# The last sample's store behind the section, and SyncE's closing waits in a section of their own

## The chip, the cores and the metric

The kernel runs on one core of a Trainium2 chip. The core has a matrix engine (TensorE), a vector engine (VectorE), a scalar engine (ScalarE), GpSimd and SyncE, which issues transfers and waits. Each engine runs its own instruction stream; semaphores order them against each other. Transfers between the chip's memory and the core's on-chip memory (SBUF) run on 16 DMA engines. The metric is the time of one execution on the device in microseconds (us); lower is better. The kernel before takes 327.56 us, the median of three runs (327.24 to 327.79).

## What is computed

`x` has 128 samples of 128 channels by 1024 time steps in float32. Each sample names one of eight subjects, and each subject has a 128 x 128 weight matrix. Every sample is multiplied by its subject's matrix, and the product is added to the sample:

```python
def _L0_cond_ref(x, subjects, weights):
    B, C, D, T, N_SUBJECTS = (128, 128, 128, 1024, 8)
    w = weights[subjects]
    out = jnp.einsum('bct,bcd->bdt', x, w)
    return out
x = x + _L0_cond_ref(x, itok_B_0_7, L0_cond_weights)
```

A sample is 512 KB. Some 67 MB are read and 67 MB written, whatever the kernel does.

## The kernel before

The kernel is written in one block, a critical section, in which every semaphore and every wait is set by hand. The layer around it (the tile context) adds what stands before and behind a section: at the end of a section SyncE raises a mark, every other engine drains and raises a count, and SyncE collects these counts; at the end of the program all engines meet twice in a barrier.

Work goes in tiles of four samples (`H * G`, two pairs of two), so there are `NT` = 32 tiles. Twelve tiles (`SLOTS`) can be held in SBUF at once; tile i uses slot i mod 12. A unit of work is one pair, but for the first pair, which is taken sample by sample.

- SyncE issues the loads (`load`, L123), one 512 KB transfer for each sample, in order. From tile 12 on it first waits until the slot's last store has landed (L171).
- GpSimd copies each sample's weight matrix into one of four small buffers (L202); the first copy of a pair also waits for the pair's loads.
- TensorE multiplies (L212): two matmuls of 512 columns for each sample, each recorded as two instructions, a pair into one of two PSUM buffers.
- VectorE adds the product to the sample in place, in SBUF (L223), and raises `s_added`.
- ScalarE waits for `s_added` and issues the stores (`store`, L56 is the line that records each transfer of either kind). Tile 0 is stored in three pieces, every other tile in one transfer of 2 MB when its second pair is done. So tile 31 goes as one transfer of 2 MB, sent when the very last addition is done.

Each slot has two semaphores, `s_pair[k][0]` and `s_pair[k][1]`. Loads and stores raise them by 16 for each transfer; `emptied` and `loaded` work out the values to wait for. A tile's store raises the second one.

At the end of the section SyncE waits until the last twelve tiles' stores have landed (L233). In the profile these waits stand on L233, the closing of the section on L141 (SyncE's branch out of the section, its mark, everybody's drain, SyncE's collection) and the end of the program on L257 (the two barriers and the clearing of the semaphores between them). The order of the instructions on each engine is the order in which they are written here; no scheduler moves anything inside the section.

Of the kernel before, what the change touches and what calls it, by code (L numbers as in the profile page):

```python
# [26 lines left out]
G = 2  # L30
H = 2
# [3 lines left out]
SLOTS = 12  # L35
# [5 lines left out]
DMA = 16  # L41
# [7 lines left out]
def transfer(nc, engine, out, in_):  # L49

    later, nc._always_lower_symbolic_ap = nc._always_lower_symbolic_ap, False
    ins, outs = engine.lower_ap_dma(in_), engine.lower_ap_dma(out)
    nc._always_lower_symbolic_ap = later
    return engine.add_instruction(  # L56
        mybir.InstDMACopy(
            name=nc.get_next_instruction_name(),
            engine=engine.engine,
            ins=ins,  # L60
            outs=outs,
            mode="Copy",
            cce_op=ALU.bypass,
            queue=QUEUES[engine.engine],
        )
    )


@with_exitstack
def kernel(  # L70
    ctx: ExitStack,
    tc: tile.TileContext,
    x: bass.AP,
    subjects: bass.AP,
    weights: bass.AP,
    out: bass.AP,
):
    nc = tc.nc
    B, C, T = x.shape
    S, _, D = weights.shape  # L80
    NT = B // (G * H)

    def sbuf(name, *shape, dtype=F32):
        return ctx.enter_context(nc.sbuf_tensor(name, list(shape), dtype)).ap()

    given, near, wrap, index = (
        sbuf(name, 1, B, dtype=I32) for name in ("given", "near", "wrap", "index")
    )
    w_all = sbuf("w_all", C, S, D)
    ws = [sbuf(f"w{i}", C, 1, D) for i in range(W_SLOTS)]  # L90
    zeros = sbuf("zeros", C, N)
    xs = [sbuf(f"x{i}", C, H * G, T) for i in range(SLOTS)]
    ps = [
        ctx.enter_context(nc.psum_tensor(f"ps{i}", [D, G, T], F32)).ap() for i in range(P_SLOTS)
    ]

    s_given = tc.alloc_semaphore("s_given")
    s_wall = tc.alloc_semaphore("s_wall")
    s_index = tc.alloc_semaphore("s_index")
    s_zeros = tc.alloc_semaphore("s_zeros")  # L100
    s_copied = tc.alloc_semaphore("s_copied")
    s_product = tc.alloc_semaphore("s_product")
    s_added = tc.alloc_semaphore("s_added")

    s_pair = [[tc.alloc_semaphore(f"s_pair{i}_{h}") for h in range(H)] for i in range(SLOTS)]


    s_first = tc.alloc_semaphore("s_first")

    def emptied(i, h):  # L110


        turns = i // SLOTS
        return (DMA * G + (DMA if h == H - 1 else 0)) * turns

    def loaded(i, q):

        if i + q == 0:
            return s_first, DMA
        h = q // G  # L120
        return s_pair[i % SLOTS][h], emptied(i, h) + (DMA if i + h == 0 else DMA * G)

    def load(engine, i, q):  # L123
        k, h = i % SLOTS, q // G
        transfer(
            nc,
            engine,
            xs[k][:, q, :],
            x[i * H * G + q].rearrange("(a r) t -> a (r t)", r=ROWS),
        ).then_inc(s_first if i + q == 0 else s_pair[k][h], DMA)  # L130

    def store(i, q0, q1):
        k, b = i % SLOTS, i * H * G
        transfer(
            nc,
            nc.scalar,
            out[b + q0 : b + q1].rearrange("g d t -> d g t"),
            xs[k][:, q0:q1, :].rearrange("d (o g) t -> d o (g t)", g=min(G, q1 - q0)),
        ).then_inc(s_first if i + q1 == 1 else s_pair[k][(q1 - 1) // G], DMA)

    with tc.tile_critical():  # L141

        nc.scalar.dma_start(given, subjects.rearrange("(o b) -> o b", o=1)).then_inc(s_given, DMA)

        nc.vector.memset(zeros, 0.0).then_inc(s_zeros, 1)  # L145
        nc.tensor.wait_ge(s_zeros, 1)
        for _ in range(IDLE):
            nc.tensor.matmul(  # L148
                ps[P_SLOTS - 1][:, G - 1, :N], zeros[:, :D], zeros, start=True, stop=True
            )  # L150

        nc.vector.wait_ge(s_given, DMA)
        nc.vector.tensor_scalar(near, given, -S, S - 1, ALU.max, ALU.min).then_inc(s_index, 1)  # L155
        nc.vector.wait_ge(s_index, 1)
        nc.vector.tensor_scalar(wrap, near, 0, S, ALU.is_lt, ALU.mult).then_inc(s_index, 1)  # L157
        nc.vector.wait_ge(s_index, 2)
        nc.vector.tensor_tensor(index, near, wrap, ALU.add).then_inc(s_index, 1)  # L159
        nc.gpsimd.wait_ge(s_index, 3)  # L160


        load(nc.sync, 0, 0)
        nc.sync.dma_start(w_all, weights.rearrange("s c d -> c s d")).then_inc(s_wall, DMA)
        for i in range(NT):
            k = i % SLOTS
            if i == SLOTS:
                nc.sync.wait_ge(s_first, 2 * DMA)
                nc.sync.wait_ge(s_pair[0][0], emptied(i, 0))
            if i >= SLOTS:  # L170
                nc.sync.wait_ge(s_pair[k][H - 1], emptied(i, H - 1))  # L171
            for q in range(H * G):
                if i + q:
                    load(nc.sync, i, q)


        units = [(0, g, g + 1) for g in range(G)]
        units += [(j // H, j % H * G, (j % H + 1) * G) for j in range(1, NT * H)]
        for u, (i, q0, q1) in enumerate(units):
            k, j = i % SLOTS, i * H + q0 // G  # L180
            p = ps[j % P_SLOTS]

            ahead = j < P_SLOTS
            if ahead:
                nc.tensor.wait_ge(*loaded(i, q0))
            for q in range(q0, q1):
                b = i * H * G + q
                if b % R == 0:  # L190
                    _, subject = nc.values_load_multi_w_load_instructions(
                        index[0:1, b : b + R],
                        engines=[mybir.EngineType.Pool],
                        min_val=0,
                        max_val=S - 1,
                        skip_runtime_bounds_check_because="the index is clamped on the chip above",
                    )
                if b == 0:
                    nc.gpsimd.wait_ge(s_wall, DMA)
                if not ahead and q == q0:  # L200
                    nc.gpsimd.wait_ge(s_added, u - P_SLOTS + 1)
                copy = nc.gpsimd.tensor_copy(  # L202
                    ws[b % W_SLOTS], w_all[:, bass.ds(subject[b % R], 1), :]
                )
                if not ahead and q == q0:
                    copy.wait_op(*loaded(i, q0), "sem-ge")
            copy.then_inc(s_copied, 1)

            nc.tensor.wait_ge(s_copied, u + 1)
            for q in range(q0, q1):  # L210
                for t in range(0, T, N):
                    mm = nc.tensor.matmul(  # L212
                        p[:, q % G, t : t + N],
                        ws[(i * H * G + q) % W_SLOTS][:, 0, :],
                        xs[k][:, q, t : t + N],
                        start=True,
                        stop=True,
                    )
            mm.then_inc(s_product, 1)

            mine = xs[k][:, q0:q1, :]
            nc.vector.wait_ge(s_product, u + 1)
            nc.vector.tensor_tensor(  # L223
                mine, p[:, q0 % G : q0 % G + q1 - q0, :], mine, ALU.add
            ).then_inc(s_added, 1)

            if i == 0 or q1 == H * G:
                nc.scalar.wait_ge(s_added, u + 1)
                store(i, q0 if i == 0 else 0, q1)


        for i in range(NT - SLOTS, NT):
            nc.sync.wait_ge(s_pair[i % SLOTS][H - 1], emptied(i + SLOTS, H - 1))  # L233


# [25 lines left out]
```

## Time and profile before

| | |
|---|---|
| median of the runs | 327.56 us (327.24 to 327.79, three runs) |
| the profiled execution | 327.34 us |
| its span, first to last instruction | 325.6 us |
| DMA, mean over the span | 134.85 MB, 414 GB/s |
| last load issued by SyncE | 260.8 us after the start |
| last addition on VectorE | 276.1 to 278.4 us |
| last store issued by ScalarE | 295.1 us |
| a 2 MB store, issue to landing | 46.4 us (median) |
| a matmul of 512 columns; an addition of a pair | 605 ns; 2259 ns |

The span is counted from the program's first instruction to its last; what lies around it (1.8 us here) is the same kind of work for every program. A store's time to landing is long because hundreds of transfers' pieces stand in the same queues: it is time in a queue, and not the time that the bytes take. From 278.4 us on no engine computes: what is left of the span is stores that are still queued, and the end of the program.

### The profile page before, as it was taken

The page shows a single profiled execution, that of the slowest core. Times are in us where ns is not written, and L with a number is a line of the kernel's source. Part 1 is how long each engine was busy: PE and PEld are TensorE (multiplying, and loading weights), DVE is VectorE, ACT ScalarE, POOL GpSimd, SP SyncE. Part 2 cuts the span into 40 slices and gives each one's busy share as a digit, 9 for nine tenths or more (in the row PEclk, how much of TensorE's full clock was granted, in tenths as well). Part 3 has the DMA queues.
Part 4 walks back from the last instruction along what each step waited for, and adds up shares of the span by engine and source line. Part 5 has one row for each costly group of instructions (what it writes and reads, how often), then busy time and mean ns, then how long its engine had stood idle before and what let it go on. Part 6 is the DMA issues. An engine that isn't in the chain of part 4 may idle for free.

```text
span 325.6 us, 1600 instructions
## 1 busy us (share of the span) xinstructions
PE 240.8 (74%) x518; PEld 94.5 (29%) x518; DVE 148.0 (45%) x69; POOL 34.3 (11%) x132
## 2 busy tenths in 40 slices
PE   7999988898888887888988888888888858000000
PEld 3444333333333332333333333333333323000000
DVE  1466655555555555454555555555554453200000
POOL 1011111011111111111011111111111010000000
PEclk9999999999999999999999999999999999755555
DMA  6999999999999999999999999999999999999994
GB/s 242 400 435 416 427 416 427 433 426 420 425 430 426 417 428 425 430 419 425 427 424 423 420 434 422 426 427 426 425 422 434 413 428 426 426 428 426 428 425 199
DMA packets 16058, 134.85 MB, mean 414 GB/s; under 512 B 2609, under 2 KB 3634, under 8 KB 3890
## 3 DMA queue, kind: packets, MB, share of 16 engines
q1 hardware_dynamic: 7184, 67.64, 49.7%
q10 hardware_dynamic: 8866, 67.11, 49.1%
q8 instruction: 4, 0.07, 0.1%
q14 instruction: 4, 0.03, 0.0%
HBM read 67.63 MB, written 67.11 MB: 414 GB/s over the span
## 4 chain that ended last, share of the span: by engine, by line
PE 41%; DVE 21%; issue 18%; POOL 5%; POOLq 1%; DVEq 0%; SPq 0%
PE ps L212 40%; DVE x L223 21%; POOL w L202 5%; PE ps L148 2%; POOLq L202 1%; DVE zeros L145 0%; DVEq L257 0%; SPq L141 0%
## 5 line engine op out<-in xcount | busy, mean ns | idle before, releaser
L212 PE MATMUL ps<-x,w 128*128 128x512 f32 x512 | 235.5, 605 | 33.6 <-POOL w L202 33.6
L223 DVE TENSOR_TENSOR x<-ps,x 128x2048 f32<-128x2048 f32 (+1 forms) x65 | 146.8, 2259 | 128.7 <-PE ps L212 128.7
L212 PEld LDWEIGHTS ps<-x,w 128*128 128x128 f32 x512 | 92.7, 190 | 177.0 <-issue 93.6
L202 POOL COPY w<-w_all 128x128 f32 x128 | 34.1, 296 | 237.8 <-DMA x<-in_x_dram 217.1
L148 PE MATMUL ps<-zeros 128*128 128x512 f32 x6 | 5.5, 1088 | 1.7 <-DVE zeros L145 1.7
L148 PEld LDWEIGHTS ps<-zeros 128*128 128x128 f32 x6 | 1.8, 328 | 3.7 <-issue 2.1
L145 DVE MEMSET zeros<- 128x512 f32 x1 | 0.5, 485 | 1.1 <-SPq L141 1.1
L155 DVE TENSOR_SCALAR near<-given 1x128 int32<-1x128 int32 x1 | 0.2, 214 | 0.5 <-DMA given<-in_itok_B_dram 0.5
L159 DVE CUSTOM_DVE_ANT_0 index<-near,wrap 1x256 uint16<-1x256 uint16 x1 | 0.3, 280 | 0.0
L157 DVE TENSOR_SCALAR wrap<-near 1x128 int32<-1x128 int32 x1 | 0.2, 216 | 0.0
L248 POOL MEMSET const-float32-0.0<- 128x1 f32 x1 | 0.1, 99 | 0.2 <-issue 0.2
L248 POOL MEMSET const-bfloat16-1.0<- 128x1 bf16 x1 | 0.1, 102 | 0.0
L248 POOL MEMSET const-uint8-127<- 128x1 uint8 x1 | 0.1, 102 | 0.0
L248 POOL MEMSET const-float32-1.0<- 128x1 f32 x1 | 0.1, 99 | 0.0
## 6 DMA issues: line engine op xcount, KB each, us to landing
x<-in_x_dram SPq DMA_DIRECT2D x128, 512.0 KB, 32.1
out_dram<-x ACTq DMA_DIRECT2D x31, 2048.0 KB, 46.4
out_dram<-x ACTq DMA_DIRECT2D x2, 512.0 KB, 11.8
out_dram<-x ACTq DMA_DIRECT2D x1, 1024.0 KB, 14.9
w_all<-in_L_cond_weights_dram SPq DMA_DIRECT2D x1, 512.0 KB, 4.8
given<-in_itok_B_dram ACTq DMA_DIRECT2D x1, 0.5 KB
```

The costliest lines, as they stand in the source:

```text
L145: nc.vector.memset(zeros, 0.0).then_inc(s_zeros, 1)
L148: nc.tensor.matmul(ps[P_SLOTS - 1][:, G - 1, :N], zeros[:, :D], zeros, start=True, stop=True)
L155: nc.vector.tensor_scalar(near, given, -S, S - 1, ALU.max, ALU.min).then_inc(s_index, 1)
L157: nc.vector.tensor_scalar(wrap, near, 0, S, ALU.is_lt, ALU.mult).then_inc(s_index, 1)
L159: nc.vector.tensor_tensor(index, near, wrap, ALU.add).then_inc(s_index, 1)
L202: copy = nc.gpsimd.tensor_copy(ws[b % W_SLOTS], w_all[:, bass.ds(subject[b % R], 1), :])
L212: mm = nc.tensor.matmul(p[:, q % G, t : t + N], ws[(i * H * G + q) % W_SLOTS][:, 0, :], xs[k][:, q, t : t + N], start=True, stop=True,)
L223: nc.vector.tensor_tensor(mine, p[:, q0 % G : q0 % G + q1 - q0, :], mine, ALU.add).then_inc(s_added, 1)
L248: nc = _bacc.Bacc("TRN2", target_bir_lowering=False, num_devices=1)
```

## The change

There are three edits. The last tile is no longer stored in one transfer: its first pair goes when that pair is done (1 MB), the third sample goes by itself (512 KB), and the fourth sample, sample 127, isn't stored in the section. SyncE's waits for the stores leave the first section and become a second section, `waits`, with one wait more for the last tile's first pair. Sample 127 is stored by a `dma_start` of ScalarE outside both sections, so that its semaphore belongs to the tile context, and the end of the program waits for it. A dependence for the scheduler alone says on which side of `waits` it stands.

```diff
-            if i == 0 or q1 == H * G:
+            if i == 0 or q1 == H * G or i == NT - 1:
                 nc.scalar.wait_ge(s_added, u + 1)
-                store(i, q0 if i == 0 else 0, q1)
-
-
+                store(i, q0 if i in (0, NT - 1) else 0, q1 - (b == B - 1))
+
+
+
+    with tc.tile_critical() as waits:
         for i in range(NT - SLOTS, NT):
             nc.sync.wait_ge(s_pair[i % SLOTS][H - 1], emptied(i + SLOTS, H - 1))
+        nc.sync.wait_ge(s_pair[(NT - 1) % SLOTS][0], emptied(NT - 1 + SLOTS, 0) + DMA)
+    last = nc.scalar.dma_start(out[B - 1], xs[(NT - 1) % SLOTS][:, H * G - 1, :])
+
+    tc.add_manual_dep(
+        last.ins,
+        waits.name,
+        mybir.DependencyInfo(mybir.DependencyClass.NoSync, mybir.DependencyReason.SCHED_ONLY),
+        reason="the end of the program waits for it",
+    )
```

In the built program the instructions stand as follows. SyncE: loads, the closing of the first section, the waits for stores (those of tiles 20 to 30, of the last tile's first pair and of sample 126), the closing of the second section, one drain that waits for sample 127's semaphore, the barriers. ScalarE: its stores, the drain that closes the first section, the store of sample 127 behind a wait for SyncE's count that the first section is closed, the barriers. The other engines pass one more branch.

## The prediction

> **What bounds the kernel now.** I read the page first (span, the row of DMA shares, the queues), then a table of windows over the last 26 us, then SyncE's list of waits, then the instructions of the three lines that end the program.
>
> ```profile
> span 325.6 us, 1600 instructions
> ...
> PE 240.8 (74%) x518; PEld 94.5 (29%) x518; DVE 148.0 (45%) x69; POOL 34.3 (11%) x132
> ...
> DMA  6999999999999999999999999999999999999994
> ...
> q1 hardware_dynamic: 7184, 67.64, 49.7%
> q10 hardware_dynamic: 8866, 67.11, 49.1%
> q8 instruction: 4, 0.07, 0.1%
> q14 instruction: 4, 0.03, 0.0%
> ```
>
> No engine is full, but the 16 DMA engines are busy in every slice except the first and the last: q1 (SyncE's loads) and q10 (ScalarE's stores) together take 98.8% of their span. The kernel is bound by its bytes. The change moves no bytes away, so it can gain only where the DMA engines are not full: at the very end.
>
> ```profile
> core 0: us, PE busy (x) PEld busy (x) DVE busy (x) POOL busy (x), PEclk, DMA share, GB/s
> 300.00:319.00 19.00, 0.00 (x0) 0.00 (x0) 0.00 (x0) 0.00 (x0) 0.50 1.01 426
> ...
> 320.30:321.20 0.90, 0.00 (x0) 0.00 (x0) 0.00 (x0) 0.00 (x0) 0.50 0.57 237
> 321.20:322.40 1.20, 0.00 (x0) 0.00 (x0) 0.00 (x0) 0.00 (x0) 0.50 0.29 123
> 322.40:323.60 1.20, 0.00 (x0) 0.00 (x0) 0.00 (x0) 0.00 (x0) 0.50 0.06 27
> 323.65:325.56 1.91, 0.00 (x0) 0.00 (x0) 0.00 (x0) 0.00 (x0) 0.50 0.00 0
> ```
>
> Compute is over; stores alone run at 426 GB/s until 320.3. Then the 16 engines run dry one after another: a share of 0.06 (1 of 16) from 322.4 to 323.6 is a single last engine. For the last 1.91 us nothing moves: that is the tail the change works on.
>
> ```profile
> L233 SPq EVENT_SEMAPHORE  x6: 17/28/28, 299.5 to 324.1; - x6
> ...
> L141 SPq EVENT_SEMAPHORE  x3: 17/28/28, 324.3 to 324.5; - x3
> L141 SPq COMPARE_BRANCH  x1: 38/38/38, 324.1 to 324.1; - x1
> L141 SPq DRAIN  x1: 7/7/7, 324.4 to 324.4; - x1
> L141 SPq NOP  x1: 18/18/18, 324.6 to 324.6; - x1
> ...
> L257 SPq DRAIN  x3: 7/7/7, 324.6 to 324.9; - x3
> L257 SPq EVENT_SEMAPHORE  x2: 17/17/17, 324.8 to 325.5; - x2
> ...
> SPq L233 <- DMA out_dram<-x: 62.4, 6, 38.0
> ```
>
> SyncE sits in its waits for stores (L233, 62.4 us) until 324.1; only then does it close the section (L141) and enter the program's end (L257). In the trace's records with more digits: the last DMA packet ends at 323.638, the last of the store's sixteen increments lands at 324.034 (the fifteenth at 322.742), SyncE's wait runs at 324.051, the branch at 324.118, its mark 324.283, its drain 324.369, its collection of the other engines 324.448, 324.508 and 324.574, a drain 324.632, and the drain that reports to the end's barrier 324.695. The span ends at 325.560.
>
> **The skill.** "DMA: Bandwidth & Descriptors", Why a DMA increments its semaphore by 16 and not by 1: the engines of one DMA finish independently and only the full 16 means landed. The trace agrees: sixteen increments over 3.3 us. Same page, Anatomy of one DMA: most of a DMA's fixed cost is the receipt of its last write, about 2 us in all. Here last packet to increment is 0.40 us; I use that. "Perfetto Trace Analysis", Sequencer-only Instruction (DRAIN, etc): the profiler shows the execution alone, neither the wait ahead nor the propagation behind. The trace agrees: durations of 7 to 38 ns, but starts 58 to 165 ns apart. So I price steps by distance between starts.
>
> **The change, part by part.** The built programs show the order on each engine.
>
> *Removed from the path: closing the section.* Before, all of 324.051 to 324.695, 0.644 us, comes after the last landing. In the new program SyncE passes section one behind its last load (261) once ScalarE has issued its stores, waits in the second section for everything but the last sample, closes it, and then stands in one drain that waits for the last store's semaphore. Behind that landing come only this wake (17 ns, as before) and one step to the barrier's drain (324.632 to 324.695, 0.063). Removed: 0.644 - 0.063 = 0.581 us. The barrier (324.695 to 325.560, 0.865) is the same on all engines and stays.
>
> *The second section must be done by then.* It wakes on the landing of sample 126. One sample is 8 packets of 4 KB on each engine; packets of 4 KB take 0.159 us in the trace and overlap by 0.004, so 8 x 0.155 + 0.006 for the increment = 1.25 us before the last landing. SyncE then has six further waits already met (six steps of 0.066, from 324.508 to 324.574: 0.40), the branch (0.07), its mark (0.17), drain (0.09), a NOP on its own count (0.08, estimate from the neighbouring steps) and one more (0.06): 0.87. Slack: 0.38 us, so it is hidden. If it weren't, each 0.1 beyond the slack takes 0.1 off the gain.
>
> *Added: issuing the last store late.* It stands on ScalarE behind the drain that closes section one and waits for SyncE's count 3, given once all engines have drained. Nothing is queued behind it but the end's barrier. ScalarE's issue of the present last store runs from 295.1 to 301.5, held back by a full queue. The closing exchange costs under 0.6 (as above), the issue 0.5 (least of the rows of stores, 507 ns), so the last store is queued by about 303; even a wait as long as the longest issue (14.3) ends at 316. DMA engines need it at 322.4 (last engine) and at 319.1 (first). Cost 0, by the cover of some 20 us of queued stores. Without this cover the price is that of the third rival.
>
> *Changed packets.* Samples 126 and 127 leave as 4 KB packets instead of 8 KB ones: 16 x 0.155 = 2.480 for 8 x 0.307 = 2.456 per engine, plus two more increments of 0.006: +0.04 us on the last landing. Bounds 0 and 0.1.
>
> *Nothing:* the wait on the first pair's semaphore (met long before); the first pair's earlier issue condition (ScalarE is behind anyhow); SyncE's extra instructions, which run in the 60 us in which it only waits.
>
> Sum: -0.581 + 0.04 = -0.54 us, from 327.34 of the profiled execution (its span plus 1.78 around it, unchanged) to 326.80; the median shown is 0.22 higher, so 327.56 - 0.54 = **327.0**. This is 0.16%. A measurement of this kernel tells about 0.2%, 0.655 us, from no change: three runs before spread over 0.55.
>
> **Rivals.**
> *A larger gain, 326.3.* The end hangs on one DMA engine 1.29 us behind the next. Instructions are fetched over the same engines: q8's 4 packets take about 1.0 us each in the records, q14's 0.31. The new program shifts every engine's blocks by 1 to 8 instructions; if one fetch less falls to the last engine, or is placed elsewhere, 0.31 to 1.05 comes on top: 0.85 to 1.6 in all. Against: programs grow rather than shrink, and the last fetch (247) is far from the end.
> *A wait in place of the one removed, 327.5.* The second section closes later than the last landing; that takes steps of 0.87 + 0.38 + 0.54 = 1.8 us instead of 0.87. Against: each step has its neighbour in the trace.
> *Slower, 328.5.* ScalarE's drain ahead of the last store could hold until its earlier stores have landed; no drain in this trace stands behind a DMA in flight, so it isn't excluded. The store would then go out at sample 126's landing (322.8) plus the exchange (0.2): issue at 323.0, first packet 0.89 later (as with the index load: issued 0.92, first packet 1.81), 8 packets 1.25, receipt 0.40: landing at 325.6 instead of 324.03. +1.5 - 0.58 = +0.96. It decides when the issue falls behind about 321.5; below that the queue never runs dry. Against: the drains shown take 7 to 41 ns, and loads and stores have explicit semaphores.
>
> **How the numbers follow.** Forecast 0.70, own range 326.7 to 327.35 from the packets' bounds and the runs' spread; its centre lies short of the 0.2% limit, so 0.34 of it beyond and 0.36 within. Larger gain 0.17, all beyond. No gain 0.05, within. Slower 0.08. So faster 0.51, same 0.41, slower 0.08. The range 326.2 to 327.6 leaves out the slower rival and the far end of the larger gain.
>
> **What would show it.** Right: SyncE's last section closes before the last landing; from the last landing to the end of the span 0.95 us instead of 1.53; the last store queued around 303; its packets without a gap behind sample 126's. Wrong: a gap in the DMA share ahead of the last store, ScalarE's drain lasting microseconds, a section that closes behind the landing, or a last engine whose packets end other than at 323.6 to 323.75.

## The result and the profile after

The changed kernel takes 326.69 us in the median (326.35 to 327.57, 22 runs), the kernel before 327.24 in runs beside it (326.70 to 327.79, 22 runs). The medians lie 0.55 us apart. The ratio is 0.9986 with a 95% interval of 0.9979 to 0.9992: 0.14% less, which of 327.24 us is some 0.46 us (0.26 to 0.69). A second set of runs gave 0.9988 (0.9981 to 0.9995). The profiled execution took 326.62 us.

The page of the changed kernel, its span, the row of DMA shares and the two queues:

```profile
span 324.8 us, 1609 instructions
...
DMA  7999999999999999999999999999999999999995
...
q1 hardware_dynamic: 7184, 67.64, 49.9%
q10 hardware_dynamic: 9026, 67.11, 49.2%
q8 instruction: 4, 0.07, 0.1%
q14 instruction: 4, 0.03, 0.0%
```

The bytes are the same; the store queue has 160 packets more (8 KB packets cut into 4 KB ones, and two more sets of 16 increments). The instruction fetches are the same in number. The DMA engines are as full as before, up to the same place. The windows over the end:

```profile
core 0: us, PE busy (x) PEld busy (x) DVE busy (x) POOL busy (x), PEclk, DMA share, GB/s
300.00:319.00 19.00, 0.00 (x0) 0.00 (x0) 0.00 (x0) 0.00 (x0) 0.50 1.01 425
320.30:321.20 0.90, 0.00 (x0) 0.00 (x0) 0.00 (x0) 0.00 (x0) 0.50 0.67 273
321.20:322.40 1.20, 0.00 (x0) 0.00 (x0) 0.00 (x0) 0.00 (x0) 0.50 0.31 126
322.40:323.40 1.00, 0.00 (x0) 0.00 (x0) 0.00 (x0) 0.00 (x0) 0.50 0.09 37
323.50:324.84 1.34, 0.00 (x0) 0.00 (x0) 0.00 (x0) 0.00 (x0) 0.50 0.00 0
```

The stores run without a break up to 320.3 and the engines run dry one after another, as before. What has become shorter is the stretch behind: in the windows 1.34 us with nothing on the wires where it was 1.91 us, and from the last packet's end to the end of the span 1.37 where it was 1.92. Where the section's closing went, by the instructions of its lines (L142 closes the first section, L236 waits for stores, L234 closes the second section, L238 is the last store, L269 is the end; the last five of SyncE's waits and its branch, 322.8 to 323.1, are recorded on L269 too):

```profile
L142 ACTq DRAIN  x1: 398/398/398, 303.8 to 303.8; - x1
...
L238 ACTq DMA_DIRECT2D out_dram<-x x1: 545/545/545, 304.3 to 304.3; - x1
...
L236 SPq EVENT_SEMAPHORE  x4: 28/28/28, 314.0 to 322.7; - x4
...
L234 SPq NOP  x2: 13/13/13, 304.3 to 323.4; - x2
L234 SPq EVENT_SEMAPHORE  x1: 17/17/17, 323.2 to 323.2; - x1
L234 SPq DRAIN  x1: 7/7/7, 323.3 to 323.3; - x1
...
L269 SPq DRAIN  x3: 7/7/7, 323.9 to 324.2; - x3
```

In time order: ScalarE drains at 303.8 and issues the last store at 304.3, some 15 us before the first DMA engine reaches it and 18 us before the last one does. (The drain is ScalarE's part in closing the first section.) SyncE closes the second section at 323.2 to 323.4, while the last store's packets are still moving, and stands in the end's drain until the last landing, 323.9. SyncE's waits say the same in one line:

```profile
SPq L269 <- DMA out_dram<-x: 0.5, 1, 0.5
```

SyncE comes to the end's drain 0.5 us early and waits there for the last store. A store has landed when the last of its sixteen semaphore increments has come; from the last landing to the end of the span is what I call the tail. In the records with more digits, the two stand like this in every kernel of this study (its runs are told below):

| kernel | last packet ends | last landing | end of span | landing to end |
|---|---|---|---|---|
| before | 323.638 | 324.034 | 325.560 | 1.526 |
| changed | 323.472 | 323.891 | 324.845 | 0.954 |
| split alone | 324.054 | 324.436 | 326.021 | 1.585 |
| whole tile behind | 323.397 | 323.796 | 324.751 | 0.955 |
| second closing added | 323.004 | 323.402 | 325.573 | 2.171 |
| last store unqueued | 325.051 | 325.417 | 326.372 | 0.955 |
| thin cover | 324.476 | 324.896 | 326.084 | 1.188 |
| thin cover, wait first | 324.015 | 324.419 | 325.930 | 1.511 |
| fifteen engines | 325.350 | 325.704 | 326.703 | 0.999 |
| changed, again | 323.350 | 323.769 | 324.723 | 0.954 |
| whole tile, again | 323.321 | 323.720 | 324.674 | 0.954 |

The last column is what the change works on, and equal programs give it to a nanosecond. The landing itself is not so steady: the kernel before and the one with a second closing do the same up to there, and land at 324.03 and 323.40; and the 22 runs of the changed kernel lie 1.2 us apart. So spans of single executions can't settle a gain of 0.5 us, but the last column and many runs can.

### The profile page after: what moved, and what is told of

It is laid out like the page before. It is cut to its first block, busy times and chain, and to the rows that moved or that the text cites. A ratio compares the mean times of both kernels' runs of the same rounds, so it can differ in the third digit from the quotient of the medians.

```text
span 324.8 us, 1609 instructions
## 1 busy us (share of the span) xinstructions
PE 241.5 (74%) x518; PEld 94.8 (29%) x518; DVE 148.0 (46%) x69; POOL 34.3 (11%) x132
## 4 chain that ended last, share of the span: by engine, by line
PE 40%; DVE 21%; issue 17%; POOL 4%; DMA 2%; POOLq 1%; SPq 1%
PE ps L213 40%; DVE x L224 21%; POOL w L203 4%; DMA x<-in_x_dram 2%; POOLq L203 1%; SPq L57 1%; SPq L165 0%; SPq L269 0%; SPq L142 0%
## 5 line engine op out<-in xcount | busy, mean ns | idle before, releaser
L149 PE MATMUL ps<-zeros 128*128 128x512 f32 x6 | 4.6, 927 | 1.7 <-DVE zeros L146 1.7
L260 POOL MEMSET const-float32-0.0<- 128x1 f32 x1 | 0.1, 99 | 0.2 <-issue 0.2
L260 POOL MEMSET const-bfloat16-1.0<- 128x1 bf16 x1 | 0.1, 102 | 0.0
L260 POOL MEMSET const-uint8-127<- 128x1 uint8 x1 | 0.1, 102 | 0.0
L260 POOL MEMSET const-float32-1.0<- 128x1 f32 x1 | 0.1, 99 | 0.0
```

Source lines behind the costliest of these rows:

```text
L149: nc.tensor.matmul(ps[P_SLOTS - 1][:, G - 1, :N], zeros[:, :D], zeros, start=True, stop=True)
L260: nc = _bacc.Bacc("TRN2", target_bir_lowering=False, num_devices=1)
```

## The experiments

**The split without the second section.** The last tile leaves in its three pieces, but in the first section, and the waits stay there too.

```diff
+            if i == 0 or q1 == H * G or i == NT - 1:
+                store(i, q0 if i in (0, NT - 1) else 0, q1 - (b == B - 1))
+                if b == B - 1:
+                    store(i, q1 - 1, q1)
...
+        nc.sync.wait_ge(s_pair[(NT - 1) % SLOTS][0], emptied(NT - 1 + SLOTS, 0) + DMA)
```

> The last tile leaves in the same three pieces (1 MB, 512 KB, 512 KB), but all of them and all waits are in the one section of the kernel before. Theory (the gain is the closing of the section taken from behind the last landing): no gain, +0.04 us for the 4 KB packets, ratio 1.000 to before; from the last landing to the end 1.53 us as before. Rival (the gain comes from splitting the last store, which lands sooner): about -0.5 us, ratio 0.9985, with the tail still 1.53 us.

Measured: 1.0003 (0.9994 to 1.0011). The closing stands behind the landing again (SyncE's instructions of L141, with the landing at 324.44):

```profile
L141 SPq EVENT_SEMAPHORE  x3: 17/28/28, 324.7 to 325.0; - x3
L141 SPq NOP  x2: 13/16/18, 0.7 to 325.0; - x2
L141 SPq COMPARE_BRANCH  x1: 38/38/38, 324.6 to 324.6; - x1
```

The tail is 1.585 us, 0.06 longer than before, because the added wait stands behind the wait that is met last: one more step. Splitting the last store gains nothing: 0.9985, which it would have given as the cause, lies outside the interval.

**The second section without the split.** The last tile leaves in one 2 MB store as in the kernel before, behind the section.

```diff
-                store(i, q0 if i == 0 else 0, q1)
+                if i < NT - 1:
+                    store(i, q0 if i == 0 else 0, q1)
...
+    with tc.tile_critical() as waits:
+        for i in range(NT - SLOTS, NT - 1):
...
+    last = transfer(
+        nc,
+        nc.scalar,
+        out[B - H * G : B].rearrange("g d t -> d g t"),
+        xs[(NT - 1) % SLOTS].rearrange("d (o g) t -> d o (g t)", g=G),
+    )
```

> No split: the last tile leaves in one 2 MB store as before (8 KB packets), but this store stands behind the section and SyncE's waits for the other tiles are the second section. Theory: the whole gain is here without the split, -0.58 us against before (0.04 better than the changed kernel), ratio 0.9982; SyncE's second section closes some 4 us ahead of the last landing, and the tail is 0.95 us. Rival (the split is needed): ratio 1.000.

Measured: 0.9981 (0.9971 to 0.9990), tail 0.955. SyncE's closing of its second section (L235) and the end (L274):

```profile
L235 SPq NOP  x2: 13/13/13, 295.3 to 319.6; - x2
L235 SPq EVENT_SEMAPHORE  x1: 17/17/17, 319.4 to 319.4; - x1
...
L274 SPq DRAIN  x3: 7/7/7, 323.8 to 324.1; - x3
```

It closes at 319.6, 4.2 us ahead of the landing at 323.8. The whole gain is here without any split: what counts is that the end's own drain waits for the last store. Beside the changed kernel it was run once more:

> The changed kernel once more, beside the next one: ratio 0.9985 to before, tail 0.95 us.

> The last tile's one 2 MB store behind the section, once more, beside the changed kernel: 0.04 us less than the changed kernel if the 4 KB packets are all that tells them apart, ratio 0.998 to before; the difference is below what these runs can tell, so only the tail (0.95 us) and the last engine's 32 packets of 8 KB for the tile count.

0.9988 (0.9981 to 0.9995) for the changed kernel and 0.9989 (0.9981 to 0.9997) for the whole tile: these runs don't tell the two apart.

**The suspected cost twice.** The kernel before, with a second section that holds one wait met long ago.

```diff
+    with tc.tile_critical():
+        nc.sync.wait_ge(s_given, DMA)
```

> The kernel before with one more section behind the first, which holds only a wait that is met from the start. Theory (closing a section behind the last landing is paid in full): the tail grows by one more closing, 0.071 + 3 x 0.06 + 0.065 + 0.165 + 0.089 + 0.074 = 0.64 us as the steps stand in the changed kernel's trace, to 2.17 us; ratio 1.0020. Rival (the closing is cheap, and the tail is the barriers): tail below 1.7 us, ratio 1.000.

Measured: 1.0022 (1.0013 to 1.0031), tail 2.171 us, 0.645 more than before. SyncE's two closings (L141, then L235) and the end (L260), with the landing at 323.40:

```profile
L141 SPq COMPARE_BRANCH  x1: 38/38/38, 323.5 to 323.5; - x1
L141 SPq DRAIN  x1: 7/7/7, 323.7 to 323.7; - x1
...
L235 SPq EVENT_SEMAPHORE  x1: 17/17/17, 324.4 to 324.4; - x1
L235 SPq DRAIN  x1: 7/7/7, 324.5 to 324.5; - x1
...
L260 SPq DRAIN  x3: 7/7/7, 324.6 to 325.0; - x3
```

Each instruction is recorded with 7 to 38 ns, yet the closing adds 645 ns: it is paid by the distance from one start to the next.

**The last store with the queue run dry.** The price of the prediction's slower rival: ScalarE waits for sample 126's landing before the first section closes.

```diff
+        nc.scalar.wait_ge(s_pair[(NT - 1) % SLOTS][H - 1], emptied(NT - 1 + SLOTS, H - 1))
     with tc.tile_critical() as waits:
```

> The changed kernel, with ScalarE made to wait at the end of the first section until sample 126's store has landed, so that sample 127's store goes out with the queue dry. Prediction's third rival gives the price: landing of sample 127 about 1.5 us later than in the changed kernel, tail 0.95 us, so +1.5 us against the changed kernel and +0.96 against before, ratio 1.003 to before. If issuing behind the section costs nothing even when the queue is dry: ratio 0.9985 as the changed kernel.

Measured: 1.0037 (1.0023 to 1.0050), 328.52 us. The windows, then the last store (L239):

```profile
322.70:323.50 0.80, 0.00 (x0) 0.00 (x0) 0.00 (x0) 0.00 (x0) 0.50 0.00 0
323.50:325.10 1.60, 0.00 (x0) 0.00 (x0) 0.00 (x0) 0.00 (x0) 0.50 0.81 328
...
L239 ACTq DMA_DIRECT2D out_dram<-x x1: 388/388/388, 322.7 to 322.7; - x1
DMA to landing us min/median/max: 2.7/2.7/2.7
```

From the issue on, some 0.9 us pass before the first packet (322.73 to 323.61), and 2.7 us to the landing. ScalarE woke on sample 126 at 322.444, and sample 127 landed at 325.417: 2.97 us between them, where in the changed kernel the landings are 1.254 apart (322.637 and 323.891). So the dry queue costs 1.7 us and outweighs the 0.57 gained. The tail is 0.955 here too: the kernel is slower for the store's lateness alone.

**A thinner cover.** Only 64 KB, the last 128 time steps of sample 127, are left behind the section.

```diff
+                    transfer(
+                        nc, nc.scalar, out[b][:, : T - LAST], xs[k][:, H * G - 1, : T - LAST]
+                    ).then_inc(s_first, DMA)
...
+    with tc.tile_critical() as waits:
+        nc.sync.wait_ge(s_first, 3 * DMA)
...
+        out[B - 1][:, T - LAST :], xs[(NT - 1) % SLOTS][:, H * G - 1, T - LAST :]
```

> The changed kernel, but the store behind the section is only the last 128 time steps of sample 127 (64 KB, 8 packets of 512 B on each engine, about 0.2 us); its first 896 steps are stored in the section. Theory (the second section, 0.77 us in the changed kernel's trace, is hidden only because 1.25 us of packets cover it): the cover is too thin by about 0.6 us, SyncE closes the section behind the last landing, and the tail from the last landing to the end is 0.95 + 0.6 = 1.55 us; the gain is gone, ratio 1.000 to before. Rival (any store behind the section will do, whatever its size): tail 0.95 us, ratio 0.9985.

Measured: 0.9992 (0.9982 to 1.0001), tail 1.188 us. The ratio fits either expectation; the tail decides. The cover, the time in which the last store is still in flight, is too thin, but by 0.23 us and not by 0.6. Its records: the piece in the section lands at 324.704, the last one at 324.896. SyncE's wait for the former is the last of its waits, and from there its steps took 0.43 us to the end's drain. I had charged the 0.77 us of the changed kernel, where six further waits, all met long before, stand behind the one that is met last. The program puts the waits in an order of its own (two to an instruction, from the middle of the list outwards), so I moved this wait from the head of the list in the source to its end, and in the built program five waits came to stand behind it:

> As the thin cover (last 128 time steps of sample 127 behind the section), but SyncE's wait on the piece before it stands ahead of five waits that are long met, in place of last. The thin cover's tail was 1.19 us, not 1.55, and the reading is that the wait met last stood last, so that the steps behind it took 0.43 us and not 0.77. If so: five steps of 0.061 us come back, tail 1.19 + 0.30 = 1.49 us, ratio 1.000 to before. If the order of waits doesn't matter: tail 1.19 us.

Measured: tail 1.511 us, ratio 1.0004 (0.9995 to 1.0012). SyncE's closing (L239) and the end (L277) of the two, thin cover first, then the wait moved:

```profile
L239 SPq NOP  x2: 13/13/13, 306.4 to 325.1; - x2
...
L277 SPq DRAIN  x3: 7/7/7, 325.1 to 325.5; - x3
```

```profile
L239 SPq NOP  x2: 13/13/13, 306.0 to 324.9; - x2
...
L277 SPq DRAIN  x3: 7/7/7, 325.0 to 325.3; - x3
```

The landings are 324.90 and 324.42, so the end's drain is reached 0.25 us behind the landing in the one and 0.57 us in the other. The order of waits is worth 0.32 us (five steps of 0.06, 0.30). The cover must be thicker than the steps behind the last-met wait, and in the changed kernel it is.

**The last engine.** What is left beside the tail is the running dry: 3.1 us from the first of the 16 engines to the last. I tried to take work from the last engine by cutting sample 127's store into 8 and 120 rows.

```diff
+    source = xs[(NT - 1) % SLOTS][:, H * G - 1, :]
+    for last in (
+        nc.scalar.dma_start(out[B - 1][:8], source[:8]),
+        nc.scalar.dma_start(out[B - 1][8:], source[8:]),
...
```

> The changed kernel, with sample 127's store cut into channels 0 to 7 (one packet on each of eight engines) and channels 8 to 127 (120 rows, which can be shared by 15 engines, not by 16). What is left of the run dry is the spread of the 16 engines, 3.1 us from the first to the last. If the last engine is the one that is left out: its landing comes 1.25 us earlier, the end follows the second engine (0.6 us earlier), ratio 0.9968 to before. If it is another engine: last landing as in the changed kernel or 0.16 us later, ratio 0.9985 to 0.999.

Measured: 1.0009 (1.0000 to 1.0017), slower than either case. The last engine was not the one left out: in the records it carries a packet of the small piece as well as eight of the large one. That costs it one packet of 0.16 us and SyncE one more wait (tail 0.999). The rest I can't place: in the profile two packets on that engine took 404 and 436 ns in place of 159, 0.52 us in all, in one execution. By their place in time they are the last two of sample 126's store, ahead of both pieces; whether they come with the cut was not tried. A second variant, which was to give eight of the engines twelve rows each and the other eight four, gave no result, so which engines lag stays open.

## Why the prediction was right

The forecast was 0.54 us less and 327.0 us. The medians differ by 0.55 us and the ratio says some 0.46 us; the second set's medians differ by 0.28 us and its ratio says some 0.39 (0.16 to 0.62). So the size is confirmed within these intervals, and the agreement to a hundredth of a microsecond is luck. The time itself, 326.69, lies 0.3 us under the forecast 327.0, at the edge of the case's own range: the forecast started from a median of three runs, 327.56, and the same kernel's 22 runs have 327.24. What shows the mechanism is the tail, piece by piece; the forecast's own case came true, and neither the larger gain nor a slower time.

- *Removed: 0.581 us.* Measured 1.526 - 0.954 = 0.572. The wake took 17 ns, the step to the barrier 63 ns, as taken over from before; the barrier took 0.874 in place of 0.865 (its drain and its clearing of semaphores are a few ns longer). The doubling shows it from the other side (0.645 for one more section), the two halves of the change show that it is the section and not the split. Single profiles can't tell how far the last landing itself moved.
- *The second section is hidden.* Its cover was forecast as 1.25 us and measured as 1.254. Its steps, forecast as 0.87, took 0.755 from the wake (322.654) to its last instruction (323.409), and some 0.05 more to the end's drain by the steps of the doubled closing. The slack is then some 0.44 in place of 0.38: the six waits took 0.36 in place of 0.40, and the steps behind them 0.44 in place of 0.47. That the cover is what hides it is shown by the thin cover. The one wrong use of this term was in that experiment, where I carried the six waits along to a kernel in which they no longer stand behind the last one.
- *The last store is early enough.* Forecast as queued "by about 303", measured: issued at 304.3, queued at 304.8. Two terms were too small: the issue of sample 126's store was held by the full queue until 303.7, and ScalarE's drain behind a store just issued took 0.398 us, not some 10 ns. With some 15 us of queued stores ahead of it on the first engine, neither matters.
- *4 KB packets, +0.04 us.* On the last engine the two samples took 2.496 us (320.967 to 323.463); eight 8 KB packets before took 2.457 (321.172 to 323.629): +0.039.
- *The larger gain.* It rested on a fetch less on the last engine, or one placed elsewhere. The fetches on both queues are 4 and 4, as before. The records don't name the engine, so a fetch placed elsewhere can't be excluded; but 0.85 us or more lies outside both intervals. The last engine's lag behind the next was 0.64 us in the changed kernel's profile and 0.94 in that of the same kernel again, so it isn't the program alone that sets it.
- *The slower rival.* ScalarE's drain does not wait for its stores to land: it ended at 304.2, and the stores in front landed up to 322.6. Its price was forecast as 1.5 us of lateness and +0.96 on the time (1.5 - 0.58 is 0.92; with the 0.04 of the packets it comes to 0.96). When made to happen, it was 1.7 and 328.52 against 327.40, +1.1: issue to landing took 2.69 in place of 0.89 + 1.25 + 0.40 = 2.54, and the exchange ahead 0.29 in place of 0.2.

One sign that the prediction named for being wrong did appear: the last packets end at 323.47 and, in the same kernel again, at 323.35, and not at 323.6 to 323.75. The sign was badly chosen, for it took one profile's end as steady. The kernel with a second closing does the same as the kernel before up to there, and its last packets end at 323.00 where the other's end at 323.64.

The prediction gave 0.51 to a gain of more than 0.2% and 0.41 to less, and the less likely came. With 0.54 us so close to 0.2%, which side it would fall on could not be foreseen. The interval leaves out a ratio of 1; its middle lies inside 0.2%, its lower end, 0.9979, just outside.

## What to carry to other kernels

When a kernel is bound by its transfers, look at what stands between the last landing and the end: here 1.5 us, of which 0.6 was a section closed by an exchange between engines. Let the last transfer be waited for by the end of the program itself, and do every other wait and exchange while it is in flight; it needs only to take longer than the steps that stand behind the wait before it, and to be queued before the queue runs dry. Read in the built program which wait stands last, and see that it is the one that is met last; in the kernels here the end of the list in the source was not the end in the program. Price such steps by the distance between their starts, never by their durations. What is won is a fixed sum at the end, here 0.57 us of 327.

## What was not expected

- A drain costs time behind a transfer just issued: 0.398 us on ScalarE behind the stores and 0.295 us on SyncE behind the loads, and 0.141 us on ScalarE behind the last store, against 7 to 8 ns on these two engines when nothing was issued just before it. None of the three waited for a landing; what they do wait for isn't shown.
- One of the 16 DMA engines lands last, 0.6 to 1.4 us behind the next in the kernels with equal shares, and the first is done some 3 us before it. This lag isn't made by the last stores: in the kernel before it is 1.29 to 1.38 us in each of the eleven stores that land from 274 us on, and in the changed kernel 0.57 to 0.69. Where the queue had run dry, all sixteen landed sample 127 within 0.19 us. So the lag is carried along from earlier, and isn't slowness in these stores; it is the largest idle stretch left, and where it comes from wasn't settled.
